# Two transformer layers on one core: fewer steps in the chains between attention blocks

## The chip, the core and the metric

The kernel runs on one core of one Trainium2 chip. A core has a matrix engine (TensorE, PE in the profile; its weight loads are PEld), a vector engine (VectorE, DVE), an engine for functions of one element (ScalarE, ACT), a general one (GpSimd, POOL) and a queue that issues transfers (SyncE, SP). Each engine works through its own list of instructions in the order in which the program wrote them, and waits for the others by semaphores. The metric is the device time of one execution in microseconds; lower is better.

## The reference

The input is x with 2048 rows of 256 values, a context of 1601 rows and a mask of 2048 x 2048. Two layers follow each other; both have 16 heads of 16 values.

```python
# layer 0: halves x0, x1 of x; shift, scale and gate come from two rows of the context
x0 = x0 + g_msa * mha(mod(ln(x0)));  x1 = x1 + g_msa * mha(mod(ln(x1)))     # stage 0
ox = attend(qx, ky, vy) @ proj;      oy = attend(qy, kx, vx) @ proj          # stage 1, crossed halves
x  = x + g_mca * concat(ox, oy)
x  = x + g_mlp * (gelu(mod(ln(x)) @ fc1 + b1) @ fc2 + b2)
# layer 1
x = ln(x + mha(x, x, x, mask));  x = ln(x + mha(x, context, context))        # stages 2 and 3
x = ln(x + relu(x @ w1 + b1) @ w2 + b2)
```

An attention is softmax(q k / 4) v for each head, with the largest score of a row subtracted before the exponential. Everything is in 32-bit floats.

## The kernel before

**Units and steps.** The 2048 rows are four blocks of 512, and the 16 heads four groups of four. A unit is one stage, one block and one group; the blocks of stage 2 and 3 see all keys, those of stages 0 and 1 only one half ("slot") of them. The first block of stage 2 is split: its four groups first run over slot 0 (part 0) and then over slot 1 (part 1), and the two halves are merged afterwards. `stream` walks over all units in steps of one weight tile pair: each step computes one piece of the row maxima of a coming unit (L843 on TensorE, L858 or, masked, L851 on VectorE), the scores of this unit with the maxima subtracted (L921, L928, and L936 for the mask), their exponential on ScalarE (L941), and a piece of the product with the values (L957). There are 1440 such steps in all and 20 before them that make maxima alone. In this text steps are numbered with these 20 counted.

**Chains.** What lies between two attentions of a block is a chain, a Python generator: `chain_self` (stage 0 to 1), `chain_cross` (stage 1 to 2, with the Gelu MLP), `chain_masked` (stage 2 to 3), `chain_last` (after stage 3, with the Relu MLP) and `chain_context` (keys and values of the context). A chain projects (L459), normalizes (L319 to L328), transposes (L343), runs the MLP (L513 and L535), makes values (L415) and, split into a high and a low part, queries and keys (L385, L392, L393). These go through DRAM: they are written out (L397, L440) and loaded back by group (L704, L718, L752).

**How a chain gets its turn.** One chain is in work at a time. After each step of the stream the first chain in `background` is advanced by one of its own steps. A chain step is a matmul piece that takes a PSUM bank ("BANK"; left out in a step in which other work needs the bank), or what follows it, and `yield n` lets n steps pass, so that another engine can finish. `chain_after` puts a chain in the list when the sums of the last group of its block are copied, to start nine steps later. If the stream needs something that its chain hasn't made yet, `ensure` advances the chain there and then until it's made, with nothing of the stream in between.

**Division.** A unit's result is divided by the sums of its weights: three steps after the copy of the sums (L989) VectorE takes the reciprocal (L1021), two transfers through DRAM spread it over the rows (`to_rows`), and seven steps after the copy GpSimd multiplies (L1035). For part 1 of the split block `fetch_first` loads the other half and its factor at the same time, and GpSimd adds the two (L1038, L1039).

**Buffers that matter.** "hi", "lo", "sums", "u", "rd_first" and "first" share three tiles (`half`); "xn", "v", "w_raw" and "c" share two (`stage`); the eight tiles of the hidden layer are `hidden`. The next stage's attention weights are loaded by `load_attn` at the end of a stage's last chain: two loads of w_raw, copied by GpSimd (L225), w_v and bv. Loads of keys and values that aren't needed at once are issued one a step (`load_ready`). The mask comes in pieces of 128 x 512 integers (L785) that GpSimd turns into a bias (L786), two buffers for the pieces.

**The MLP.** The first layer makes eight tiles, each in two chain steps: matmuls, then ScalarE adds the bias. While the stream runs the Gelu isn't applied there, since exponential and Gelu need different tables: all eight tiles get it in a row once the eighth is made (L527), and one step passes. The second layer has two pieces, each four chain steps of four matmuls and one that adds the result.

## Time and profile before

| | before |
|---|---|
| median of 3 runs | 3405.86 us (3405.11 to 3409.05) |
| the profiled execution | 3407.57 us |
| its span, first to last instruction | 3405.8 us |
| mean granted TensorE clock | 0.968 |
| TensorE idle at L957 after the Gelus, ended by ScalarE's exponential, in each of the first three cross chains | 2.6 us |
| L385 at 1400, where `ensure` advances a chain / elsewhere, two matmuls of 512 | 3.78 us / 1.98 us |
| a bare step of stage 1 / with one chain insertion | 1.47 us / 3.58 us |

The page gives the busy time of each engine, the span in 40 slices with the clock that TensorE was granted, and the chain of work that ended last. A line of the timeline has the start, the length, the engine, the line of the kernel, what is written and read, and in square brackets how long the engine had been idle before it and what ended that. A matmul in 32-bit floats leaves two records, so "x8" is four matmuls. "PEld ... issue" is time in which nothing that the profile shows was waited for. The releaser of a wait is inferred: where a wait is for several things, the one that came last is named.

### The profile page before, as it was taken

What the parts mean: (1) busy time and instruction counts of PE and PEld (TensorE: products, weight loads), DVE (VectorE), ACT (ScalarE), POOL (GpSimd) and SP (SyncE); (2) the same over time, 40 slices, a digit from 0 to 9 for tenths busy, and PEclk for the clock granted to TensorE, in tenths of its full rate; (3) what the DMA queues carried; (4) which work ended last, traced back from release to release, by engine and by line L of the source; (5) the groups of instructions that cost most, each with busy time, mean ns of one, the idle gap of its engine ahead of it and who ended that gap; (6) DMA issues with size and microseconds to landing.
All of it is one profiled execution on the core that took longest, in us unless ns stands there. A gap on an engine that the chain in (4) does not pass through costs nothing.

```text
span 3405.8 us, 56583 instructions
## 1 busy us (share of the span) xinstructions
PE 3096.5 (91%) x22447; PEld 1359.0 (40%) x22592; DVE 2118.3 (62%) x3858; ACT 1713.7 (50%) x1868; POOL 404.1 (12%) x344
## 2 busy tenths in 40 slices
PE   4899998999999999798899999999999999999995
PEld 2334444433444443333333343333344444444443
DVE  2676766765565566366677777777657747657451
ACT  1365654655564545243455555554555645546461
POOL 0001101101010120204012001201001011110112
PEclk8799999999999999899999999999999999999997
DMA  5662152142113421343111001102241000000000
GB/s 182 142 99 65 36 104 76 44 107 57 51 34 77 77 72 32 83 111 114 32 38 56 17 23 49 43 17 54 42 77 62 26 11 26 24 18 26 10 14 16
DMA packets 162362, 191.20 MB, mean 56 GB/s; under 512 B 82584, under 2 KB 95520, under 8 KB 162096
## 3 DMA queue, kind: packets, MB, share of 16 engines
q1 hardware_dynamic: 162096, 187.57, 22.5%
q8 instruction: 178, 2.92, 0.4%
q14 instruction: 88, 0.72, 0.1%
HBM read 129.91 MB, written 48.46 MB: 52 GB/s over the span
## 4 chain that ended last, share of the span: by engine, by line
PE 75%; DVE 9%; ACT 6%; DMA 4%; issue 2%; SPq 2%; POOL 1%; ACTq 0%; DVEq 0%; POOLq 0%
PE m_ps L957 19%; PE s_ps L921 13%; PE s_ps L843 12%; PE s_ps L928 8%; PE s_ps L936 6%; ACT e L941 5%; PE m_ps L513 3%; DVE pm L858 3%; PE m_ps L535 3%; PE m_ps L385 3%; DVE s_ps L851 2%; PE m_ps L459 2%; PE m_ps L415 2%; PE m_ps L882 1%; DVE t L328 1%
## 5 line engine op out<-in xcount | busy, mean ns | idle before, releaser
L941 ACT ACTIVATE e<-s_ps 128x1024 f32<-128x1024 f32 (+1 forms) x1440 | 1466.9, 1024 | 1376.5 <-PE s_ps L928 791.6
L858 DVE TENSOR_REDUCE pm<-s_ps 128x2 f32<-128x1024 f32 (+3 forms) x1024 | 1117.3, 1105 | 533.4 <-PE s_ps L843 529.7
L957 PE MATMUL m_ps<-e,V 128*32 128x256 f32 (+2 forms) x10432 | 903.3, 417 | 15.1 <-ACT e L941 8.0
L851 DVE CUSTOM_DVE_ANT_0 s_ps<-s_ps,bias 128x512 f32<-128x512 f32 x1024 | 713.2, 701 | 295.7 <-PE s_ps L843 160.1
L843 PE MATMUL s_ps<-kT,q 64*128 64x512 f32 (+3 forms) x3072 | 679.9, 445 | 105.2 <-ACT e L941 53.1
L921 PE MATMUL s_ps<-q,kT 64*128 64x512 f32 (+1 forms) x2880 | 676.6, 466 | 62.6 <-DVE pm L858 23.9
L928 PE MATMUL s_ps<-nm,sel 64*128 64x512 f32 (+1 forms) x2880 | 575.2, 395 | 0.1
L843 PEld LDWEIGHTS s_ps<-kT,q 64*128 64x128 f32 x3072 | 293.6, 186 | 530.3 <-issue 310.1
L921 PEld LDWEIGHTS s_ps<-q,kT 64*128 64x128 f32 (+1 forms) x2880 | 270.5, 184 | 504.1 <-issue 241.2
L957 PEld LDWEIGHTS m_ps<-e,V 128*32 128x32 f32 (+1 forms) x10432 | 207.0, 108 | 439.7 <-issue 412.2
L936 PE MATMUL s_ps<-biasT,ident 128*128 128x512 bf16 x879 | 278.4, 385 | 23.3 <-issue 23.3
L1035 POOL TENSOR_TENSOR oT<-oT,rd_rows 64x512 f32<-64x512 f32 x64 | 81.6, 1275 | 1766.8 <-DMA rd_rows<-rd_dr 1476.1
L928 PEld LDWEIGHTS s_ps<-nm,sel 64*128 64x128 f32 (+1 forms) x2880 | 275.3, 187 | 12.2 <-ACT nm L887 0.8
L786 POOL TENSOR_SCALAR bias<-raw 128x512 bf16<-128x512 int32 x64 | 123.0, 1922 | 287.9 <-DMA raw<-in_mask 269.6
L851 DVE DVE_READ_ACCUMULATOR2_ANT pm<- 128x1 f32 x1024 | 144.8, 141 | 0.0
L936 PEld LDWEIGHTS <-ident 128*128 128x128 bf16 x1024 | 58.3, 97 | 187.7 <-issue 187.7
L393 DVE SCALAR_TENSOR_TENSOR lo<-m_ps,qkb,hi 128x512 fp32r<-128x512 f32 (+2 forms) x56 | 41.1, 734 | 140.9 <-ACT hi L392 112.5
L385 PE MATMUL m_ps<-hT,w_qk 128*128 128x512 f32 (+2 forms) x224 | 116.2, 644 | 11.8 <-DVE lo L393 10.7
L535 PE MATMUL m_ps<-w_mlp,hid 128*128 128x256 f32 x448 | 115.1, 401 | 0.0
L513 PE MATMUL m_ps<-hT,w_mlp 128*128 128x512 f32 x224 | 111.0, 618 | 0.7 <-ACT hT L358 0.7
L535 PEld LDWEIGHTS m_ps<-w_mlp,hid 128*128 128x128 f32 x448 | 83.2, 195 | 30.9 <-issue 20.0
L392 ACT ACTIVATE hi<-m_ps,qkb 128x512 fp32r<-128x512 f32 (+2 forms) x56 | 37.8, 674 | 80.8 <-PE m_ps L385 69.2
(106 smaller groups left out, 1237.0 us busy)
## 6 DMA issues: line engine op xcount, KB each, us to landing
q<-q_dr SPq DMA_DIRECT2D x544, 64.0 KB
kT<-k_dr SPq DMA_DIRECT2D x192, 128.0 KB
raw<-in_mask SPq DMA_DIRECT2D x64, 256.0 KB
q_dr<-hi SPq DMA_DIRECT2D x32, 256.0 KB
q_dr<-lo SPq DMA_DIRECT2D x32, 256.0 KB
oT<-sums SPq DMA_DIRECT2D x256, 32.0 KB
rd_rows<-rd_dr SPq DMA_DIRECT2D x64, 128.0 KB
v_dr<-v SPq DMA_DIRECT2D x14, 544.0 KB
```

The source lines that it names most:

```text
L385: nc.tensor.matmul(m[:, :n], lhsT=wqk[:, k, w, c, :], rhs=hT[:, k, :n], start=k == 0, stop=k == 1)
L513: nc.tensor.matmul(m, lhsT=w1[k][:, f * P : (f + 1) * P], rhs=hT[:, k, :], start=k == 0, stop=k == 1,)
L535: nc.tensor.matmul(m[:, q2 * D : (q2 + 1) * D], lhsT=hid[f][:, qt * P : (qt + 1) * P], rhs=w2[f // 4][:, f % 4, :], start=f == 0, stop=f = ...
L786: nc.gpsimd.tensor_scalar(bias_rows[b, slot, qt][:, j * BLK : (j + 1) * BLK], raw, 0.0, MASKED, ALU.is_equal, ALU.mult,)
L843: nc.tensor.matmul(s[:, h, :nn], lhsT=u["q"][64 * h : 64 * h + 64, i, qt * P : (qt + 1) * P], rhs=kT[g][slot][64 * h : 64 * h + 64, i, c : ...
L851: nc.vector.tensor_tensor_reduce(out=s[:, h, :], in0=s[:, h, :], in1=bias_rows[b, slot, qt][:, c : c + nn], scale=1.0, scalar=-3.0e38, op0 ...
L858: nc.vector.tensor_reduce(u["pm"][:, qt, :, i, n], s[:, :, :nn], AX.X, ALU.max)
L921: nc.tensor.matmul(s[:r, h, :], lhsT=kT[g][slot][64 * h : 64 * h + 64, i, kt * P : kt * P + r], rhs=u["q"][64 * h : 64 * h + 64, i, :], st ...
L928: nc.tensor.matmul(s[:r, h, :], lhsT=sel[64 * h : 64 * h + 64, i, :r], rhs=u["nm"][64 * h : 64 * h + 64, :], start=False, stop=not masked,)
L936: nc.tensor.matmul(s[:, h, :], lhsT=ident16, rhs=bias_columns[b, slot, kt], start=False, stop=True,)
L941: nc.scalar.activation(e[:r], s[:r], AF.Exp, scale=SCALE)
L957: nc.tensor.matmul(u["av"][PH * j : PH * (j + 1), cut], lhsT=V[g][slot][:r, kt * GW + j * VW : kt * GW + j * VW + PH], rhs=u["e"][n, j % 2 ...
```

## The change

It has three parts. The second layer of the MLP runs in two steps a piece, with eight matmuls each, in place of four with four. The Gelu of each tile stands right before the matmul that is the first to read it, in the first of these steps, and the step that passed after the Gelus is gone. Some waits are shorter by one step: after GpSimd's power in `normalize`, after the projection in `chain_self` and `chain_cross`, before the division, and before a chain starts (but for the split block).

```diff
@@ normalize
         nc.gpsimd.tensor_tensor(rs, ve, minus_half, ALU.pow)
-        yield 2
+        yield 1
@@ mlp
-        if wait:
-            for t in hid:
-                nc.scalar.activation(t, t, func)
-            yield 1
         if between is not None:
             between()
 
-        def down(m, n, q2, fs):
+        def down(m, n, q2):
             qt = 2 * n + q2
-            for f in fs:
+            for f in range(DFF // P):
+                if wait and qt == 0:
+                    nc.scalar.activation(hid[f], hid[f], func)
                 nc.tensor.matmul(
...
         for n in range(2):
             yield from piece(
-                *(
-                    lambda m, n=n, q2=q2, fs=fs: down(m, n, q2, fs)
-                    for q2 in range(2) for fs in (range(4), range(4, 8))
-                ),
+                *(lambda m, n=n, q2=q2: down(m, n, q2) for q2 in range(2)),
                 lambda m, n=n: finish(n, m.rearrange("p (t d) -> p t d", d=D)),
             )
@@ chain_self, chain_cross, after the projection
-        yield 3
+        yield 2
@@ chain_after
-        go = now[0] + 9
+        go = now[0] + (9 if "part" in u else 8)
@@ stream, a unit that isn't split
-                        later.append([7, lambda w=w: divide(w), False])
+                        later.append([6, lambda w=w: divide(w), False])
```

## The prediction

> **What bounds the kernel now.** I read the busy totals and slices of the page first, then the chain of work that ended last, the waits of each engine, and the timeline of every place where TensorE stood idle for over 1.5 us.

> ```profile
> PE 3096.5 (91%) x22447; PEld 1359.0 (40%) x22592; DVE 2118.3 (62%) x3858; ACT 1713.7 (50%) x1868; POOL 404.1 (12%) x344
> ...
> PEclk8799999999999999899999999999999999999997
> ...
> PE 75%; DVE 9%; ACT 6%; DMA 4%; issue 2%; SPq 2%; POOL 1%; ACTq 0%; DVEq 0%; POOLq 0%
> ```

> TensorE is busy 91% and carries 75% of the chain, so work moved on ScalarE, VectorE or GpSimd pays only where TensorE stands still. Merging its records, I find about 285 us idle, of which some 50 us lie in the first 100 us and 23 us after 3300. The rest sits in few places. The windows view (columns: length, busy time and count of PE, PEld, DVE, ACT, POOL, clock, DMA share, GB/s) shows the two worst beside a sound stretch:

> ```profile
> 1340.00:1391.00 51.00, 48.72 (x281) 23.75 (x284) 21.85 (x59) 24.77 (x30) 17.93 (x10) 1.00 0.21 55
> 1391.00:1431.00 40.00, 19.79 (x64) 9.50 (x64) 6.41 (x15) 3.88 (x6) 2.67 (x3) 0.69 0.44 100
> ...
> 1560.00:1640.00 80.00, 62.69 (x358) 27.56 (x364) 44.16 (x129) 24.91 (x31) 38.75 (x24) 0.85 0.33 95
> ```

> The first, in the timeline (start, length, engine, line, what, idle before):

> ```profile
> 1400.30 3.78 PE L385 MATMUL m_ps<-hT,w_qk 128*128 128x512 f32 x4 [0.68 <-ACT hT L358]
> ...
> 1417.10 4.09 SPq L704 DMA_DIRECT2D kT<-k_dr  x8
> ...
> 1428.01 0.76 PE L843 MATMUL s_ps<-kT,q 64*128 64x512 f32 x1 [2.93 <-DMA kT<-k_dr]
> ...
> 1430.69 1.02 ACT L941 ACTIVATE e<-s_ps 128x1024 f32<-128x1024 f32 x1 [20.41 <-PE s_ps L936]
> 1447.39 0.95 SPq L221 DMA_DIRECT2D w_raw<-in_w_attn  x2
> 1453.44 0.38 SPq L639 DMA_DIRECT2D c<-in_ctx  x1
> ```

> At step 576 the last cross chain isn't ready when its keys are needed: the program issues the remaining 13 chain steps back to back, each waiting for its own ScalarE and VectorE partner, then eight key loads, then goes on. One step takes 39.5 us. The matmul of 3.78 us is the one that takes 1.98 elsewhere: TensorE also runs at half clock.

> [...] (the load of c is issued 6.05 us after w_raw, whose buffer it reuses, and nothing passes it).

> **The change part by part.** Steps are counted in the issue order of both kernels.

> *(1) Second layer in two steps a piece.* A chain step's four logical matmuls (eight records) cost 3.58−1.47 = 2.11 us above a bare step of stage 1. In the tail 32 stand in a row in 13.83 us, so four are 1.73; 0.38 is the price of each insertion. Four insertions vanish per MLP. Six MLPs run among unmasked steps; three of these pieces hold Gelu (part 2), so 3×3+3×4 = 21 × 0.38 = **−8**. The fourth cross MLP runs in masked steps, where its insertions cover idle time (3.92−2.2 = 1.7 us for the four): 0. Bounds −8 and 0. The last chain_last runs alone; its matmul order is unchanged.

> *(2) Gelu within the first step.*

> ```profile
> 1179.07 1.28 ACT L527 ACT_TABLE_LOAD   x1
> 1180.37 4.27 ACT L527 ACTIVATE hid<-hid 128x512 f32<-128x512 f32 x8
> 1187.02 0.63 PE L957 MATMUL m_ps<-e,V 128*32 128x256 f32 x6 [2.60 <-ACT e L941]
> ...
> 1188.38 3.49 PE L535 MATMUL m_ps<-w_mlp,hid 128*128 128x256 f32 x8
> ```

> Before: three steps and two insertions take 13.54 us (1178.26 to 1191.80) instead of 3×1.47+2×2.11 = 8.63; lost 4.9. After: ScalarE's order is the step's exponential, table load, eight Gelus, table load; both loads stay. TensorE waits in the down step, with all its later scores queued behind it, for 0.1+1.02+1.28+0.61+0.1 = 3.1 us, then is paced at first by the half clock: about six tiles at 0.79 us (3.15/4, from the first MLP), two at 0.45, so 5.7 instead of 3.9. Lost 4.9: **0** over four MLPs, ±2 each, bounds −8 and +8.

> *(3) The forced run goes.* With five chain steps fewer in the MLP, two from the other waits and one from the start, chain_cross(1) has its keys at 573 and its queries at 575; nothing is forced at 576. The ten steps from 1391.22 to 1461.31 take 70.1 us; their content is 10×2.1, one old down insertion 2.1, two transposes 2, six groups of L385 or L415 at 2.1, 12.6, and 1.8 of small work: 39.5. Excess 30.6. But a new wait stands there. On SP three of ten key transfers pass at one a step; the other five key tiles now stand behind w_raw, w_v, bv and c. With t the end of the last L385: w_raw at t+2, c at t+8.1 (the 6.05 us above), the last kT at t+11, landed near t+16.5 (c takes 4.05 us from issue to use; eight kT took 10.9 us before, so five about 6). TensorE reaches L843 at t+2.4, everything behind it stops: 14 us, plus about 2.5 of half clock. Net 16.5−30.6 = **−14**; bounds −26 (loads hide) and 0.

> *(4) Context chains against the merge of the halves.*

> ```profile
> 1574.31 0.75 DVE L393 SCALAR_TENSOR_TENSOR lo<-m_ps,qkb,hi 128x512 fp32r<-128x512 f32 x1 [6.76 <-POOL first L1038]
> ...
> 1629.42 0.42 DVE L393 SCALAR_TENSOR_TENSOR lo<-m_ps,qkb,hi 128x194 fp32r<-128x194 f32 x1 [7.85 <-POOL first L1038]
> ```

> "hi", "lo", "rd_first" and "first" share three buffers. Steps 626 to 629 take 26.6 us for 4×3.92 = 15.7, step 640 takes 12.1 for 3.9: excess 19. After, context chain 2 makes its keys at 620 and 621, ahead of the merge at 623, and chain 3 at 632 and 633, ahead of that at 639. Chain 3 now meets the 16 mask loads of steps 620 to 631 on SP, each paced by GpSimd's 1.92 us plus gaps: its last "lo" needs a store queued behind them, about 8 us late, with 1.5 at c and 2 of clock: 11.5. **−7**; bounds −17 and +3.

> *(5) Chain one step earlier (9 to 8).* The projection L459 comes a step sooner and waits for the last division, which lands when its DMAs do; the division's own 7 to 6 moves no DMA, only its place on GpSimd; the chain's 512 KB load of t stays behind the division's transfers on SP.

> ```profile
> 532.42 2.93 PE L459 MATMUL m_ps<-w_p,oT 128*128 128x256 f32 x6 [5.24 <-POOL oT L1035]
> ```

> Margins from division end to L459 are mostly 2.0 to 2.7 us against steps of 1.47: no wait. Four are thin, and lose 0.5 (957), 1.5 (1119), 1.9 (2540), 1.6 (3149): +5.5. At 526 and 793 the division is late because key loads of the next stage crowd SP; those end six steps earlier, so 5.6 and 3.4 go. **−3.5**; bounds −9 and +10.

> *(6) Queries behind w_raw.* At 723 to 734, steps 316 to 319 take 13.1 us for about 7: q loads queue behind w_raw. After, six key loads stand between and q is six steps later relative to w_raw: **−5**; bounds −6 and 0.

> *(7) Shorter waits.* GpSimd's power (1.03 us) now has one VectorE reduction (1.23 us) to hide behind, its two additions (2.56 us) two steps (2.94). Hidden; uncovered, they'd cost 0.2 and 0.4 us per chain. The third cross chain's stores now share SP with eight mask loads (steps 503 to 511): "lo" waits about 1.5 us. **+2**; bounds 0 and +10.

> Sum: −8+0−14−7−3.5−5+2 = −35.5. The profiled execution took 3407.57 us, span 3405.8, the median of the runs is 3405.86: span and median agree, so 3405.8−35.5 = **3370 us**.

> **The rivals.** *The stalls only move*: key loads behind c cost as much as the forced run, and parts 3 and 4 give nothing. Left: −14.5, 3391 us. For it: SP's order. Against it: 16.5 is far from 30.6. *The loads hide*: parts 3 and 4 reach −26 and −17: 3348. For it: the DMA share is only 0.44 there. Against it: c needs w_raw landed and copied. *Slower*: the load of c is held much longer, so L843 stands for 14+35.5 = 50 us or more; that decides at 50, and at 60 gives 3416. Only GpSimd's four weight copies (1.0 us) stand between, hence unlikely. *Nothing*: the forced run recurs in another place: 3406.

> **How the numbers follow.** Chances: forecast 0.70, its own range 3352 to 3389; moved stalls 0.12; hidden loads 0.10; slower 0.04; nothing 0.04. The range 3346 to 3396 leaves out part of the tails and the last two. Within 0.2% (6.8 us) is about what a measurement of this kernel can't tell from no change: faster 0.90, same 0.05, slower 0.05.

> **What would show it.** Down groups of sixteen records, insertions near 3.8 us (1); TensorE idle about 3 us before the first of each cross MLP (2); no step of 39 us, but one near 18 with L843 waiting for kT (3); no "lo" waiting for "first" (4); L459 waits gone near 527 and 794, 1 to 4 us near 1119, 2540 and 3149 (5). I'm wrong if L843 waits over 30 us, if Gelu steps lose over 7 us each, or if idle time grows where chains ran alone.

## The result

| | before | after |
|---|---|---|
| median, 14 runs each | 3406.99 us (3398.40 to 3413.14) | 3403.58 us (3397.78 to 3416.45) |
| ratio on record, 95% interval (the medians alone give 0.9990) | | 0.9998 (0.9986 to 1.0009) |
| the profiled execution, its span | 3407.57, 3405.8 us | 3412.04, 3410.2 us |
| TensorE idle between its first and last matmul, its records merged | 292.2 us | 304.7 us |

No change that could be measured, where 3370 us were forecast. The profiled execution of after is 8.5 us above the median of its kernel, so the stretches below are read beside those of the experiments, some of which have the same code in most stages. The idle time that the prediction puts at about 285 us is 292 in this count.

The page of after, its busy totals, the clock in 40 slices and the chain that ended last:

```profile
PE 3088.3 (91%) x22447; PEld 1360.9 (40%) x22592; DVE 2121.6 (62%) x3858; ACT 1712.8 (50%) x1868; POOL 404.1 (12%) x344
...
PEclk8899999999999999899999999999999999999997
...
PE 72%; DVE 8%; ACT 7%; DMA 5%; issue 3%; SPq 3%; POOL 2%; ACTq 0%; DVEq 0%; POOLq 0%
```

TensorE carries 72% of the chain instead of 75%; DMA, SP and issue have gained three points together. Lines of the changed kernel have moved by two to four: the row maxima are L839 (TensorE) and L854 or L847 (VectorE), the scores L917 and L924, the value product L953, the Gelu L533, the second layer L534, the loads of keys L700, of queries L748, of mask pieces L781, of c L635.

The windows of after around the two places that the prediction showed (columns as there):

```profile
1423.00:1441.00 18.00, 4.28 (x21) 1.52 (x24) 3.90 (x12) 1.02 (x1) 2.21 (x9) 0.63 0.91 213
1590.00:1630.00 40.00, 27.25 (x155) 12.71 (x158) 20.71 (x67) 11.79 (x16) 18.81 (x11) 0.87 0.35 97
```

Both are still poor, the first for 18 us where it was 40. What took the place of the forced run, in the timeline of after:

```profile
1423.81 0.95 SPq L221 DMA_DIRECT2D w_raw<-in_w_attn  x2
...
1429.35 0.38 SPq L635 DMA_DIRECT2D c<-in_ctx  x1
1429.78 2.37 SPq L700 DMA_DIRECT2D kT<-k_dr  x5
...
1435.64 0.76 PE L839 MATMUL s_ps<-kT,q 64*128 64x512 f32 x1 [11.72 <-DMA kT<-k_dr]
```

The last five key loads stand behind c, which stands 5.5 us behind w_raw, and TensorE waits 11.72 us for the first of them. The Gelus, in the same view:

```profile
830.24 1.02 ACT L937 ACTIVATE e<-s_ps 128x1024 f32<-128x1024 f32 x1 [1.04 <-PE s_ps L924]
831.28 1.28 ACT L533 ACT_TABLE_LOAD   x1
832.58 4.26 ACT L533 ACTIVATE hid<-hid 128x512 f32<-128x512 f32 x8
...
833.26 5.49 PE L534 MATMUL m_ps<-w_mlp,hid 128*128 128x256 f32 x16 [3.11 <-ACT hid L533]
```

The matmuls wait 3.11 us for exponential, table and first Gelu. The merge at 1600, where "lo" waited for "first":

```profile
1599.04 4.06 SPq L748 DMA_DIRECT2D q<-q_dr  x8
...
1604.20 0.76 PE L839 MATMUL s_ps<-kT,q 64*128 64x512 f32 x1 [5.86 <-DMA q<-q_dr]
...
1615.54 0.42 DVE L393 SCALAR_TENSOR_TENSOR lo<-m_ps,qkb,hi 128x194 fp32r<-128x194 f32 x1 [7.81 <-DMA k_dr<-hi]
```

"lo" waits for a store now, and just before, TensorE waits for queries. And a projection with the chain one step earlier:

```profile
1112.51 1.77 PE L459 MATMUL m_ps<-w_p,oT 128*128 128x256 f32 x6 [2.62 <-POOL oT L1031]
```

Where the time went, by stretches between the same steps of the stream (differences to before in us, from the starts of the exponentials in the profiles; the experiments are named below). A step has the number of the exponential that opens it, which is one less than the prediction's number: its step 576 is 575 in this table and in what follows.

| steps | before | after | masks later | keys earlier | two steps after power | the same, last chains only |
|---|---|---|---|---|---|---|
| 20 to 212 | 377.6 | +0.9 | -4.9 | -3.2 | -3.1 | -2.2 |
| 212 to 404 | 432.2 | -14.8 | -14.6 | -15.9 | -17.4 | -18.5 |
| 404 to 468 | 160.6 | +6.2 | +5.4 | +3.4 | +1.5 | +5.6 |
| 468 to 540 | 184.2 | +16.8 | +7.3 | +15.4 | +9.3 | +14.3 |
| 540 to 670 | 425.7 | -10.6 | -15.4 | -23.9 | -13.7 | -15.4 |
| 670 to 1054 | 829.0 | +3.5 | +3.4 | +5.3 | -0.2 | +3.6 |
| 1054 to 1158 | 184.3 | +2.6 | +1.7 | +0.3 | +3.4 | +1.2 |
| 1158 to 1459 | 605.4 | +0.8 | +3.2 | -0.4 | -10.2 | -11.1 |

Each column is one execution, and these lie off the medians of their kernels: 8.5 us above it for after, 2.4, 7.8 and 9.3 below it for masks later, keys earlier and the last column, 3.7 above it for two steps. So a difference of a few us between two columns in one stretch says little; those on which the main readings rest are larger, or are checked against a second kernel with the same code there.

So the gain is there, at 212 to 404 and 540 to 670, and is given back at 404 to 540. And stage 3 (from 1054), where the new second layer should save 0.38 us at each of twelve insertions, saves nothing.

Two new waits stand out in the list of TensorE's idle spells. The larger, of 8.36 us, at step 507 (after):

```profile
1208.73 6.19 SPq L781 DMA_DIRECT2D raw<-in_mask  x3
1210.31 0.69 ACT L392 ACTIVATE hi<-m_ps,qkb 128x512 fp32r<-128x512 f32 x1 [1.90 <-DMA oT<-sums]
...
1215.02 0.38 SPq L397 DMA_DIRECT2D k_dr<-hi  x1
...
1218.52 0.75 DVE L393 SCALAR_TENSOR_TENSOR lo<-m_ps,qkb,hi 128x512 fp32r<-128x512 f32 x1 [9.98 <-DMA k_dr<-hi]
...
1219.33 2.93 PE L415 MATMUL m_ps<-w_v,hT 128*128 128x256 f32 x6 [8.36 <-DVE lo L393]
```

Read it upwards: the matmul waits for "lo", "lo" for a tile whose content has not been stored, and that store waits on SP behind three mask loads, which hold SP for 6.19 us; the third waits for a buffer that GpSimd empties (L782, 3.94 us for two pieces). Step 507 takes 13.85 us.

The other is small and comes six times, twice for each of three last chains (after, first of the six):

```profile
2741.16 2.34 DVE L328 TENSOR_SCALAR t<-t,mv,rs 128x256 f32<-128x256 f32 x4
...
2743.42 2.88 DVE L854 TENSOR_REDUCE pm<-s_ps 128x2 f32<-128x896 f32 x3
...
2744.55 0.43 PE L839 MATMUL s_ps<-kT,q 64*128 64x354 f32 x2 [1.78 <-DVE pm L854]
2744.91 0.77 PE L953 MATMUL m_ps<-e,V 128*32 128x256 f32 x8
...
2745.61 0.80 PE L917 MATMUL s_ps<-q,kT 64*128 64x512 f32 x2
```

The four scalings of the normalization stand on VectorE ahead of the reductions of the one step in which two pieces of maxima fall together. L839 needs a score tile that those reductions free, waits 1.78 us, and then TensorE runs at half clock: 0.80 us for what takes 0.50, with a mean clock of 0.62 from 2744.50 to 2749.00.

### The profile page after: what moved, and what is told of

Read it like the earlier page. It is cut to its first block, busy times and chain, and to the rows that moved or that the text cites. A ratio compares the mean times of both kernels' runs of the same rounds, so it can differ in the third digit from the quotient of the medians.

```text
span 3410.2 us, 56623 instructions
## 1 busy us (share of the span) xinstructions
PE 3088.3 (91%) x22447; PEld 1360.9 (40%) x22592; DVE 2121.6 (62%) x3858; ACT 1712.8 (50%) x1868; POOL 404.1 (12%) x344
## 4 chain that ended last, share of the span: by engine, by line
PE 72%; DVE 8%; ACT 7%; DMA 5%; issue 3%; SPq 3%; POOL 2%; ACTq 0%; DVEq 0%; POOLq 0%
PE m_ps L953 19%; PE s_ps L917 13%; PE s_ps L839 11%; PE s_ps L924 8%; PE s_ps L932 6%; ACT e L937 6%; PE m_ps L514 3%; PE m_ps L534 3%; DVE pm L854 3%; PE m_ps L385 2%; DVE s_ps L847 2%; PE m_ps L459 2%; PE m_ps L415 2%; PE m_ps L878 1%; DVE t L328 1%
## 5 line engine op out<-in xcount | busy, mean ns | idle before, releaser
L854 DVE TENSOR_REDUCE pm<-s_ps 128x2 f32<-128x1024 f32 (+3 forms) x1024 | 1120.4, 1106 | 533.0 <-PE s_ps L839 528.8
L953 PE MATMUL m_ps<-e,V 128*32 128x256 f32 (+2 forms) x10432 | 907.7, 419 | 10.3 <-DVE lo L393 4.5
L847 DVE CUSTOM_DVE_ANT_0 s_ps<-s_ps,bias 128x512 f32<-128x512 f32 x1024 | 713.0, 700 | 300.4 <-PE s_ps L839 166.8
L839 PE MATMUL s_ps<-kT,q 64*128 64x512 f32 (+3 forms) x3072 | 677.1, 444 | 121.3 <-ACT e L937 51.1
L917 PE MATMUL s_ps<-q,kT 64*128 64x512 f32 (+1 forms) x2880 | 677.1, 466 | 54.0 <-ACT e L937 28.4
L924 PE MATMUL s_ps<-nm,sel 64*128 64x512 f32 (+1 forms) x2880 | 575.1, 395 | 0.1
L839 PEld LDWEIGHTS s_ps<-kT,q 64*128 64x128 f32 x3072 | 293.7, 186 | 538.6 <-issue 313.8
L917 PEld LDWEIGHTS s_ps<-q,kT 64*128 64x128 f32 (+1 forms) x2880 | 270.4, 184 | 500.4 <-issue 241.7
L953 PEld LDWEIGHTS m_ps<-e,V 128*32 128x32 f32 (+1 forms) x10432 | 207.3, 108 | 437.6 <-issue 416.0
L924 PEld LDWEIGHTS s_ps<-nm,sel 64*128 64x128 f32 (+1 forms) x2880 | 275.2, 187 | 12.0 <-ACT nm L883 0.8
L782 POOL TENSOR_SCALAR bias<-raw 128x512 bf16<-128x512 int32 x64 | 123.0, 1922 | 298.4 <-DMA raw<-in_mask 276.7
L847 DVE DVE_READ_ACCUMULATOR2_ANT pm<- 128x1 f32 x1024 | 144.8, 141 | 0.0
L393 DVE SCALAR_TENSOR_TENSOR lo<-m_ps,qkb,hi 128x512 fp32r<-128x512 f32 (+2 forms) x56 | 41.1, 734 | 140.9 <-ACT hi L392 99.0
L534 PE MATMUL m_ps<-w_mlp,hid 128*128 128x256 f32 x448 | 111.2, 404 | 11.9 <-ACT hid L533 11.9
L385 PE MATMUL m_ps<-hT,w_qk 128*128 128x512 f32 (+2 forms) x224 | 111.0, 619 | 9.9 <-DVE lo L393 9.2
L534 PEld LDWEIGHTS m_ps<-w_mlp,hid 128*128 128x128 f32 x448 | 87.2, 201 | 35.4 <-ACT hid L533 14.7
```

Source lines behind the costliest of these rows:

```text
L385: nc.tensor.matmul(m[:, :n], lhsT=wqk[:, k, w, c, :], rhs=hT[:, k, :n], start=k == 0, stop=k == 1)
L534: nc.tensor.matmul(m[:, q2 * D : (q2 + 1) * D], lhsT=hid[f][:, qt * P : (qt + 1) * P], rhs=w2[f // 4][:, f % 4, :], start=f == 0, stop=f = ...
L782: nc.gpsimd.tensor_scalar(bias_rows[b, slot, qt][:, j * BLK : (j + 1) * BLK], raw, 0.0, MASKED, ALU.is_equal, ALU.mult,)
L839: nc.tensor.matmul(s[:, h, :nn], lhsT=u["q"][64 * h : 64 * h + 64, i, qt * P : (qt + 1) * P], rhs=kT[g][slot][64 * h : 64 * h + 64, i, c : ...
L847: nc.vector.tensor_tensor_reduce(out=s[:, h, :], in0=s[:, h, :], in1=bias_rows[b, slot, qt][:, c : c + nn], scale=1.0, scalar=-3.0e38, op0 ...
L854: nc.vector.tensor_reduce(u["pm"][:, qt, :, i, n], s[:, :, :nn], AX.X, ALU.max)
```

## The experiments

All ratios are to the kernel before, with 95% intervals; after has 0.9998 (0.9986 to 1.0009). Differences to after are between medians (after 3403.58 us). The kernel before was timed again beside each set of runs, with medians of 3403.6 to 3407.0 us, so a difference of medians of about 3 us between sets may be that of the sets.

**What holds the stores and the keys on SP.** Two kernels move transfers on SP in the changed kernel and leave the chains alone.

```diff
@@ mask_part
-            later.append([n, lambda n=n: mask_rows(SPLIT, slot, n // 2, n % 2), False])
+            later.append([n + 4 * (slot == 0), lambda n=n: mask_rows(SPLIT, slot, n // 2, n % 2), False])
```

> The changed kernel, with the first sixteen mask loads (raw) four steps later, so that the stores of the keys of steps 506 and 507 are issued on SP ahead of the third raw. My theory (a store held behind a waiting load on SP is what ate the gain of the cross chain): the 8.36 us for which TensorE waits at 1210.79 and the half clock after it go; steps 503 to 511 lose 10 to 12 us of the 16.8 that steps 478 to 530 gained, about 3393 us. Rival (the wait only moves): the raws then stand ahead of the query stores of steps 509 to 512, lo waits there, and the time stays within 3 us of the changed kernel's, 3401 to 3406. Second rival (bias rows late): the maxima of step 512 wait for the mask rows, and it is slower, above 3408.

Measured: 3392.85 us, ratio 0.9968 (0.9956 to 0.9981), 10.7 us below after. The same place in its timeline:

```profile
1199.91 0.53 SPq L397 DMA_DIRECT2D k_dr<-hi  x1
...
1202.25 0.75 DVE L393 SCALAR_TENSOR_TENSOR lo<-m_ps,qkb,hi 128x512 fp32r<-128x512 f32 x1 [1.80 <-ACT hi L392]
1203.06 1.59 PEld L415 LDWEIGHTS m_ps<-w_v,hT 128*128 128x128 f32 x8 [0.64 <-DVE lo L393]
1203.06 1.99 PE L415 MATMUL m_ps<-w_v,hT 128*128 128x256 f32 x8 [0.20 <-DVE lo L393]
```

The store goes out at once, the wait of 8.36 us is 0.20, and the matmuls take 1.99 us for eight records, where after has 2.93 for six. The first theory held; neither rival did.

```diff
@@ chain_cross
-        yield from keys_and_values(2, hT, b)
+        yield from keys_and_values(2, hT, b); last and load_ready([(2, 0, 1)])
```

> The changed kernel, with the ten key and value loads of the last unit of stage 2 issued as soon as the keys are stored, ahead of w_raw and c on SP. My theory (the keys wait behind w_raw and c in SP's order): the waits of 11.72 and 2.00 us before the first scores of step 576 fall to 0 to 3 together, half clock with them, minus 10 to 14 us against the changed kernel, about 3391 us. Rival (the DMA engines, not SP's order, are what is full there): the load of c comes late instead, the context chain waits for it, and less than 5 us is gained: 3399 to 3404.

Measured: 3395.05 us, ratio 0.9976 (0.9967 to 0.9984), 8.5 us below after, between the two theories. The timeline says why:

```profile
1414.52 0.46 PE L839 MATMUL s_ps<-kT,q 64*128 64x512 f32 x1 [1.55 <-DMA kT<-k_dr]
...
1423.81 0.38 SPq L635 DMA_DIRECT2D c<-in_ctx  x1
...
1429.60 0.63 PE L343 MATMUL m_ps<-identR,c 128*128 128x128 f32 x4 [2.25 <-DMA c<-in_ctx]
```

The wait for keys is 1.55 us instead of 13.7, as the first theory has it; and steps 540 to 670 take 23.9 us less than before, where two other kernels with after's code in this stretch (masks later, and two steps in the last chains) take 15.4 less: 8.5 us, the difference of the medians (after's own profile takes 10.6 less there, which would make it 13.3). A part comes back, since c is late by 2.25 us now. So the keys did wait in SP's order, and freeing them moves a smaller wait to c.

> The changed kernel with both moves on SP: mask loads four steps later and the last keys of stage 2 as soon as they are stored. They took 10.7 and 8.5 us off one by one. If the two waits are independent: 3384 us (3381 to 3388). If the transfers now crowd each other at steps 576 to 640: less than 4 us below the better one, 3389 to 3393.

Both edits together: 3383.54 us, ratio 0.9944 (0.9928 to 0.9960). The two gains add up: 10.7 + 8.5 = 19.2 us, and 20.0 measured, so the two waits are independent within the noise.

**Which part gives and which takes.** The parts alone; the first is the kernel before with after's function for the MLP, the second is after with that of before.

> The kernel before with the new second layer and Gelu alone (all waits as before). The forced run at step 576 is still there, with 8 chain steps issued in a row where the kernel before had 13. If the parts add up as forecast, merging gives minus 8, Gelu 0, and the forced run shrinks by 5 of 13 steps, about minus 8 of its 30.6 us: 3391 us. If the gains of each merged insertion (0.38 us) are lost to what the chains wait for (VectorE, stores), as the comparison of the changed kernel with the one before suggests: within 4 us of the kernel before, 3403 to 3409. No wait of 1.78 us after the power in stage 3 in either case, since two steps are left for it.

Measured: 3399.40 us, ratio 0.9988 (0.9978 to 0.9998), between both expectations. In its profile stage 3 takes 11.4 us less than before, with a clock of 1.00 from step 1054 on; but steps 404 to 540 take 10.4 us more, where queries' "hi" now waits for the transfers of a unit's sums (1084.30: L917 idle for 2.56 us behind it). The chain that ends earlier here meets other traffic on SP.

> The changed kernel with the second layer and Gelu of the kernel before: the shorter waits alone. Forced run at step 576 with 6 chain steps in a row where the kernel before had 13: about minus 12 of its 30.6 us. Projections in the stages 1 minus 3.5. Against it the six waits of 1.78 us in stage 3 (plus 8 to 11 with the clock) should stand here as in the changed kernel, if the one step after the power causes them. Sum if so: minus 5, about 3402 us. If they come from the merged second layer and not from the wait: they are missing here and the time is 3391.

Measured: 3420.66 us, ratio 1.0052 (1.0036 to 1.0069): slower, which neither theory had. Three waits of 1.78 us and three of 1.59 stand in stage 3, which takes 17.2 us more than before from step 1054 on; the stages before end level. The shorter waits alone cost 17 us. On top of the new MLP it would be 4 us by the medians, but the intervals of these two kernels overlap.

**Which of the waits.** From here every kernel is after with one thing put back.

```diff
@@ normalize
         nc.gpsimd.tensor_tensor(rs, ve, minus_half, ALU.pow)
-        yield 1
+        yield 2
```

> The changed kernel with two steps again after the power in normalize; all else as changed. In stage 3 (steps 1054 to 1459) the changed kernel takes 3.3 us more than the one before, the new second layer alone 11.4 us less: the shorter waits cost 14.7 us there. My theory: the one step after the power does it, by six waits of 1.78 us and the half clock after each. Then the six waits are gone, stage 3 takes about 11 us less than before, and the time is 3388 to 3392 us. Rival: the earlier start of the chain (8 for 9) and the earlier division do it; then the six waits remain and the time is 3400 to 3407.

Measured: 3376.68 us, ratio 0.9918 (0.9901 to 0.9934), 26.9 us below after, twice what I had expected. The six waits are gone and steps 1158 to 1459 take 11 us less, as forecast; the rest comes from stages in which I hadn't looked for it (table above: 404 to 540, and 1.0 to 1.4 us in each of three blocks from 670 to 1054).

```diff
-        go = now[0] + (9 if "part" in u else 8)
+        go = now[0] + 9
...
-    later.append([6, lambda w=w: divide(w), False])
+    later.append([7, lambda w=w: divide(w), False])
```

> The changed kernel with the chain's start and the division put back to 9 and 7 steps; the power's one step and the second layer as changed. A run of two chain steps is forced at step 576. My theory: the six waits of 1.78 us in stage 3 stay, since they come from the power's single step; the waits of 2.62 and 1.79 us before the projections at 1109 and 2540 go. If the gain of 8.3 us at steps 212 to 276 comes from the earlier start, it is lost here: 3406 to 3412 us. If it comes from the power's single step and the merged layer, it stays: 3396 to 3402.

Measured: 3386.72 us, ratio 0.9947 (0.9928 to 0.9965), below both expectations. My theory falls here: the single step after the power is kept, and yet no wait of over 1.2 us is left in steps 1158 to 1459, which take 591.9 us instead of 606.2. The single step costs only where the chain also starts at 8. Half of the gain at 212 to 276 stays (4.3 us of 8.3).

> The changed kernel with the start of the chain put back to 9 steps, and the division left at 6. If it is the start that brings the scalings L328 into the crowded step: the six waits go, the waits of L459 before the projections go too (the division has a step more), and the time is 3380 to 3387, at or below the 3386.7 of the kernel with both put back. If the earlier division is what loads VectorE and GpSimd at the wrong step: 3395 or more, with waits left in stage 3.

With the start alone put back (the first line of that diff): 3389.27 us, ratio 0.9960 (0.9944 to 0.9975), the same as with both within the intervals. So the start by itself is enough; the division put back alone was not run. The L459 waits at 1109 and 2540 are shorter but not gone (1.46 and 1.12 us for 2.62 and 1.79), and others of 3.16 us at 526 and 2.16 at 788 are back, which I had not expected; they stand where before has 5.24 and 3.05.

```diff
@@ normalize
             nc.vector.bn_stats(st[:, i, :], src[:, i, :])
-        yield 1
+        yield 2
         for i in range(TPB):
             nc.vector.bn_aggr(mv[:, i, :], st[:, i, :])
```

> The changed kernel with its single step after the power kept, and two steps instead of one after the statistics (L319), so that the four scalings L328 come one step later, as with two steps after the power. Theory A, that the scalings of 2.34 us meet the one step in which two score reductions fall: the six waits of 1.78 us go, and the time is that of the kernel with two steps after the power, 3376.7 us (3372 to 3382). Theory B, that VectorE stands waiting for GpSimd's power of 1.02 us when only one step is left for it: the six waits stay in some form and the time is 3395 us or more.

Measured: 3379.02 us, ratio 0.9920 (0.9903 to 0.9938), the same as two steps after the power. It decides between the theories: the single step is still there, and its place is harmless. Six waits of 1.48 to 1.58 us remain (behind the first the clock is 1.00, from 2722.30 to 2726.80), and steps 1158 to 1459 take 598.9 us, 7.3 less than after, where two steps after the power save 11. This is not a wait for GpSimd, as theory B has it: before the first of the six the power ends at 2718.29, and VectorE, which has no gap there, comes to the scalings only at 2719.10. It now has the aggregates of the statistics, 0.37 and 0.17 us, ahead of the crowded step's reductions.

```diff
@@ chain_last
-        yield from post_norm(rows["a3"], t)
+        yield from post_norm(rows["a3"], t, 2)
...
-        yield from post_norm(rows["m1"], t)
+        yield from post_norm(rows["m1"], t, 2)
```

The new argument is the number of steps after the power; it stays 1 elsewhere.

> The changed kernel with two steps after the power in the last chains alone (both normalizations of each); stages before as changed. Theory A, that the meeting with the score reductions is a cost of its own: the six waits of 1.78 us and the half clock after them go, steps 1158 to 1459 take 595 us instead of 606, and the time is 3403.6 minus 11, about 3393 us (3389 to 3397). The other 14 of the 25 us then come from the stages before, where the step also moves the chain against SP's transfers. Theory B, that nearly all of the 25 us come from there: 3400 to 3404. Theory C, that the six waits and the clock are worth nearly all of it: 3379 to 3384.

Measured: 3393.02 us, ratio 0.9958 (0.9944 to 0.9971), 10.6 us below after: theory A. The first of these six normalizations in the timeline of this kernel:

```profile
2723.10 3.08 DVE L854 TENSOR_REDUCE pm<-s_ps 128x2 f32<-128x896 f32 x3
...
2726.09 2.34 DVE L328 TENSOR_SCALAR t<-t,mv,rs 128x256 f32<-128x256 f32 x4
...
2728.36 1.69 DVE L854 TENSOR_REDUCE pm<-s_ps 128x2 f32<-128x708 f32 x2
...
2729.30 0.50 PE L917 MATMUL s_ps<-q,kT 64*128 64x512 f32 x2 [1.17 <-DVE pm L854]
```

The scalings now follow the crowded step's reductions instead of leading them; a wait of 1.17 us remains, and the next matmul takes 0.50. Steps 1158 to 1459 as windows, after:

```profile
2725.63:3331.83 606.20, 574.64 (x4510) 266.68 (x4508) 361.44 (x468) 336.10 (x353) 66.79 (x54) 0.98 0.07 18
```

and with two steps in the last chains:

```profile
2709.13:3303.52 594.39, 564.61 (x4514) 263.61 (x4512) 362.42 (x468) 335.81 (x354) 66.90 (x54) 1.00 0.07 19
```

The same work on VectorE (361 and 362 us), 10.0 us less of TensorE busy and a clock of 1.00 for 0.98, while TensorE's idle time falls by 1.8 us only: most of the loss was not the waiting but the slow matmuls behind it. The two executions are 28 us apart, but this stretch is not a matter of the execution: the three other profiles with after's code in it (masks later, keys earlier, both) take 605.0 to 608.6 us. The rest of the 26.9 us, some 16, is in the stages before. There the step also moves the chain against SP's transfers, and how it divides between these and VectorE was not separated.

**Together.** Both moves on SP and two steps after the power:

> The changed kernel with both moves on SP and two steps again after the power. If the power's single step costs what I think, 12 to 15 us less than both moves alone: about 3371 us. If the earlier start is what costs in stage 3: equal to both moves alone, 3381 to 3388. If two steps more per chain bring the last cross chain late again (its keys are then stored at step 575 and asked for at 576), 4 to 8 us of the gain are lost at step 576: about 3376.

Measured: 3364.68 us, ratio 0.9887 (0.9870 to 0.9904). The step is worth 18.9 us on top of the moves; the last cross chain does come late again (TensorE waits 4.61 and 2.83 us before the scores at 1396.26 and 1399.85, the second time for keys), and still it is more than I had expected. In the last chains alone the start at 9, the division at 7 and the single step, added to this:

> Both moves on SP and two steps after the power, and in the last chains alone the start of 9, the division of 7 and the single step after the power. With these the steps 1054 to 1459 took 8.8 us less (15.6 less than before, where two steps with the start of 8 took 6.8 less). If the stages are independent: 3364.7 minus 8.8, about 3356 us. If the last stage's gain came with where the stages before it had left off: 3362 to 3367.

Measured: 3359.57 us, ratio 0.9871 (0.9856 to 0.9886), 44 us below after and the fastest of all, between the two expectations. Its interval overlaps that of the kernel without this last edit.

## Why the prediction was wrong

The step that failed is part 7, "shorter waits", +2 us within 0 to +10. Its two terms measured about 11 and 19 to 27 us: the mask loads in front of the key stores 10.7 (11.5 once the keys are moved: 3395.05 less 3383.54), the missing step of each normalization 26.9 alone and 18.9 once the moves on SP are made. The forecast lacked 33.6 us (3403.58 less 3370), and these two are 30 to 38, if they add; the kernel with these two alone was not run.

- *The wait for GpSimd* was costed as latency: is the power done when VectorE wants it? It is, within 0.15 us (in after it ends at 2741.12, the reduction before the scalings at 2741.01). What was not asked is which of VectorE's other instructions the four scalings push back. They take 2.34 us, more than a step of 1.47, and in the crowded step they led two reductions of 1.08 us each that TensorE was about to need. I added up one waiting instruction and didn't name what was queued behind it, though the views for that were there. This is shown for the last chains, 10.6 us; for the other 16 us it is open how much is VectorE's and how much SP's.
- *"lo" waits about 1.5 us* at steps 503 to 511: it waited for a store for 8.36 us of TensorE. I had counted the eight loads, but not that a load which waited for its buffer (6.19 us for three) held SP for all behind it, as in the 6.05 us that part 3 counts for c.
- *Part 1*, 0.38 us per insertion: a merged step and a bare one take 5.31 + 1.47 = 6.78 us where two insertions took 2 x 3.58 = 7.16, so 0.38 was right. But it holds only where nothing else moves: with the MLP alone stage 3 gained 11.4 us against 4.6 forecast, since the waits of up to 1.3 us in before and their half clock went too (a mean clock of 0.98 to 1.00 there in before, 1.00 here), and steps 404 to 540 lost 10.4, where six insertions less should have gained 2.3. In sum this kernel gained 4.6 us, the shorter forced run included (6.5 us at 540 to 670), where 8 were forecast for part 1 alone.
- *Part 2*, Gelu at 0: right. TensorE waits 3.11 us (forecast 3.1), and the two steps take 15.63 us for 10.6, 5.0 lost (forecast 4.9, as before).
- *Part 3*, -14: the mechanism was right to the line. Step 575 went from 39.47 to 17.64 us, with 11.72 and 2.00 us for keys (forecast 14, and a step near 18). But steps 570 and 571, where "lo" waits behind nineteen transfers of queries, masks and sums on SP, take 14.4 us for 7.9, and 581 to 584 take 20.2 for 13.5, a part of which is work that was moved there. So of the 21.8 us gained at the step 8 to 9 are left.
- *Part 4*, -7: steps 626 to 628 and 639 took 34.6 us for 4 x 3.92, an excess of 19; now 631 to 633 take 24.7 for 3 x 3.92, an excess of 13 (forecast 11.5): -6. "lo" does wait for a store behind mask loads, as forecast; the 5.86 us for queries, a load of eight behind these, were not foreseen.
- *Part 5*, -3.5: the two late divisions are gone and steps 212 to 276 gain 8.3 us, more than the 5.6 forecast; with the start at 9 only 0.8 and 4.3 of it are left (division at 6 and at 7), so most of it is the start's. Against it stand step 479 with 7.9 us, where the step with the same content took 4.45 (a loss of 1.5 was forecast), and 1.8 us at 2540 (forecast 1.9, but before already waits 1.4 there, so only 0.4 is new).
- *Part 6*, -5: steps 276 to 340 gain 1.6 us in this profile, 3.3 and 5.4 in those of the two kernels with moves on SP, which are the same there.

Among the rivals was "moved stalls" (3391), which gave up parts 3 and 4 only. None had a chain that arrives a step too early in places where it ran well before. The rival that came out had 0.04, and for another reason (a forced run elsewhere). The earlier chains met other work of VectorE and SP in several stages (the waits of 8.36, 5.86 and 1.78 us above), and the bounds of part 7, 0 to +10, were set by the two meetings that I had looked at.

## What to carry to other kernels

Shortening a wait in a hand-ordered kernel doesn't only ask if the awaited thing is ready: it puts the waiting instructions at another place in their engine's list, and what the neighbours paid here was their full length there: 2.34 us of VectorE, and on SP 6.19 us of three held loads. Before the edit, write down for each engine and queue what is issued in the step that the instructions leave and in the one that they enter. If parts of a change pull a chain earlier by one step each, try them apart: here the kernel gained 14 to 27 us with either of two waits left as it was, and nothing with both shortened.
